# Where the reload of a part's outputs stands among SyncE's transfers, in the expert stage of a convolution, attention and expert-FFN kernel

## The chip, the cores and the metric

The kernel runs on one core of one Trainium2 chip. The core has TensorE (PE: matmuls and weight loads), VectorE (DVE), ScalarE (ACT), GpSimd (POOL) and SyncE (SP), and 16 DMA engines that move data between DRAM and the on-chip memories. SyncE, ScalarE and GpSimd each issue transfers on a queue of their own. The metric is the device time of one execution in microseconds (us), given as the median of several runs.

## The reference

The input x is 32 images of 56 x 56 positions with 128 channels. It goes through a normalisation, a convolution with binarised inputs and weights, windowed attention with 4 heads, and then the part that matters here, an expert layer of 64 experts. Each expert picks the 8 best tokens of each image, pools them, puts the pooled vector through two layers, and adds its output back to the tokens that it picked:

```python
vals, idx = jax.lax.top_k(probs.transpose(0, 2, 1), K)
...
pooled = jnp.einsum('bked,bke->bed', gathered, topv)
...
h = jax.nn.gelu(jnp.einsum('ebd,edh->ebh', h, weight1), approximate=False)
...
out = jnp.einsum('ebh,eho->ebo', h, weight2)
...
weighted = jnp.einsum('beo,bke->bkeo', out, topv).reshape(Bn, K * E, O)
outputs = jnp.zeros((Bn, Sn, O), dtype=x.dtype)
outputs = outputs.at[jnp.arange(Bn)[:, None], flat_idx].add(weighted)
```

A token can be picked by several experts of its image. The result is the attention's output plus these outputs. All of it is float32; the sizes are 8 tokens an expert and image, a hidden width of 512, and 128 channels in and out.

## The kernel before

The first and by far the longest stage is a software pipeline over 112 blocks (16 pairs of images, 7 blocks a pair): convolution, attention, gate logits, and per pair the choice of tokens. It writes the attention's outputs into `out` and, for every chosen token, its row into `grows` and into `share` the weights with which the experts' outputs go into that row (zero for an expert that did not pick it).

The stage that the change touches comes last. The 64 experts are done in `NQ` = 8 parts of 8. For part q these functions are called:

- `load1` (L355) and `load2` (L360) load the two weight matrices of the part's experts, 2048 KB each, into `u1` and `u2` (the profile calls both `u`). Parts 0, 2, 4, 6 and 1, 3, 5, 7 take turns on two sets of buffers, so the weights of part q+2 can only come once part q has read its own.
- `load_rows` (L1053) and `load_shares` (L1057) load `f_rows` and `f_sh`, 1024 KB each: the token rows of the part for all 16 pairs, and their weights. There are four buffers for rows and three for shares.
- `hidden` (L1064) multiplies the pooled vectors with the first weights on TensorE; VectorE copies the result to `hs`.
- `gelus` (L1081) turns `hs` on TensorE (`hT_ps`, L1076) and applies the gelu on ScalarE, 32 instructions a part.
- `outputs` (L1096) multiplies with the second weights; VectorE adds the bias (`os`, L1102), and ScalarE's queue stores the result into `eout` in DRAM (L1104, 128 KB).
- `reload` (L1111) reads `eout` back in two transfers of 64 KB, in the layout that the next step needs: experts on the partitions. The buffer is `eo`, and the profile shows it under the name `logits`, which the same memory had before. Which queue issues the reload is an argument of the function.
- `finals` (L1120) has 16 matrix products of shares and `eo` (32 matmul instructions, `fo`), VectorE adds the token rows to them (L1125), and GpSimd writes the 16 x 128 finished rows to their places in `out` by an indirect transfer for each pair (L1129, 16 a part). The writes of part q+1 to a pair come after those of part q to the same pair, since a token can be in both.

The orders of TensorE, VectorE, ScalarE and SyncE are written out by hand: each of them runs its instructions in the order of the calls, and an instruction that waits holds what is behind it on its engine. In part q TensorE has the turn of `gelus(q)`, then `finals(q - 1)`, then `outputs(q)`, then `hidden(q + 1)`. A reload waits for its store to have landed, and `fo` waits for the reload. The framework adds waits of its own: the transfers of SyncE's and ScalarE's queues take eight semaphores in turn, and each waits until the one before it on its semaphore has landed.

Up to `outputs(0)` nothing differs. Behind it the kernel before has part 0's reload on SyncE's queue and the later ones on ScalarE's, ahead of that part's gelus. Rows and shares are loaded one part ahead, with the first weights of part q+2 ahead of them and the second weights of part q+2 issued behind `outputs(q)`.

Of the kernel before, what the change touches and what calls it, by code (L numbers as in the profile page):

```python
# [30 lines left out]
def kernel(  # L31
# [15 lines left out]
    nc = tc.nc  # L47
# [10 lines left out]
    NQ = 8  # L58
# [308 lines left out]
    def main_loop(fast):  # L367
        with ExitStack() as main:
# [564 lines left out]
            for n in range(-6, N + 1):  # L933
# [34 lines left out]
                if n == N - 4:  # L968
                    parts = [Part(0, early)]
# [79 lines left out]
            def load_rows(q, n0=0, n1=NPAIR):  # L1049

                if n0 == 0:
                    rows[q] = frow.tile([P, NPAIR, P], F32, name="f_rows")
                nc.sync.dma_start(out=rows[q][:, n0:n1], in_=grows[q][:, n0:n1])  # L1053

            def load_shares(q):
                shs[q] = fsh.tile([P, NPAIR, 2, ES], F32, name="f_sh")
                nc.sync.dma_start(out=shs[q], in_=share[q])  # L1057

            def hidden(q):
                part = parts[q]  # L1060
                for g in range(q * GQ, (q + 1) * GQ):
                    hp = eps.tile([P, HF], F32, name="hp")
                    for e in range(EG):
                        nc.tensor.matmul(  # L1064
                            hp[e * B : (e + 1) * B, :], lhsT=pooled[:, g * EG + e, :],
                            rhs=part.u1[:, g * EG + e - q * EP, :], start=True, stop=True,
                        )
                    hs[g] = eh.tile([P, HF], F32, name="hs")
                    nc.vector.tensor_copy(hs[g], hp)

            def gelus(q):
                for g in range(q * GQ, (q + 1) * GQ):
                    hT_ps = eps.tile([P, NHC, P], F32, name="hT_ps")
                    hc = hs[g].rearrange("p (m c) -> p c m", c=NHC)
                    for c in range(NHC):
                        nc.tensor.transpose(hT_ps[:, c, :], hc[:, c, :], ident)  # L1076
                    hT[g] = eh.tile([P, NHC, P], F32, name="hT")
                    for c in range(NHC):
                        for e in range(EG):
                            cols = slice(e * B, (e + 1) * B)  # L1080
                            nc.scalar.activation(  # L1081
                                hT[g][:, c, cols], hT_ps[:, c, cols], AF.Gelu,
                                bias=hbias[:, g * EG + e, c : c + 1],
                            )

            def outputs(q):
                part = parts[q]
                os = eh.tile([P, GQ, P], F32, name="os")
                for g in range(q * GQ, (q + 1) * GQ):

                    op = eps.tile([P, 2, P], F32, name="op")
                    for c in range(NHC):
                        for e in range(0, EG, 2):
                            two = slice(e * B, (e + 2) * B)
                            e0 = g * EG + e - q * EP
                            nc.tensor.matmul(  # L1096
                                op[two], lhsT=hT[g][:, c, two], rhs=part.u2[:, e0 : e0 + 2, c, :],
                                start=(c == 0), stop=(c == NHC - 1),
                            )
                    for e in range(EG):  # L1100
                        one = slice(e * B, (e + 1) * B)
                        nc.vector.tensor_add(os[one, g % GQ], op[one, e % 2, :], obias[one, g])  # L1102
                es = slice(q * EP, (q + 1) * EP)
                nc.scalar.dma_start(  # L1104
                    out=eout[es].rearrange("(g e) b o -> (e b) g o", e=EG), in_=os
                )

            def reload(q, queue):
                es = slice(q * EP, (q + 1) * EP)
                for i in range(2):  # L1110
                    queue.dma_start(  # L1111
                        out=eo[i * E + es.start : i * E + es.stop],
                        in_=eout[es].rearrange("e (i n) o -> i e n o", i=2)[i],
                    )

            def finals(q):
                for a in range(0, NPAIR, FP):
                    fo = eps.tile([P, FP, P], F32, name="fo")
                    for n in range(a, a + FP):
                        nc.tensor.matmul(  # L1120
                            fo[:, n - a, :], lhsT=shs[q][:, n].rearrange("p i s -> p (i s)"),
                            rhs=eo[:, n, :], start=True, stop=True,
                        )
                    row = rows[q][:, a : a + FP]
                    nc.vector.tensor_add(row, fo, row)  # L1125


                for n in range(NPAIR):
                    put = nc.gpsimd.indirect_dma_start(  # L1129
                        out=of, out_offset=bass.IndirectOffsetOnAxis(ap=rowidx[:, n, q : q + 1], axis=0),  # L1130
                        in_=rows[q][:, n, :], in_offset=None,
                    ).ins
                    before = [last[n]] if n in last else []
                    for w in before:
                        tc.add_manual_dep(put, w.name, sync_dep, reason="rows of the same images")
                    tc.declare_no_dep(put, group=puts, keep=before, reason="rows of other images")
                    tc.add_to_no_dep_group(puts, put)
                    last[n] = put
# [30 lines left out]
            load_shares(0)  # L1169
            outputs(0)  # L1170

            hidden(1)
            reload(0, nc.sync)
            load_rows(1)
            load_shares(1)
            parts[2].load2()
            for q in range(1, NQ + 1):
                if q > 1:
                    if q < NQ:
                        hidden(q)  # L1180
                    reload(q - 1, nc.scalar)
                if q + 2 < NQ:
                    parts[q + 2].load1()
                if q + 1 < NQ:
                    load_rows(q + 1)
                    load_shares(q + 1)
                if q < NQ:
                    gelus(q)
                finals(q - 1)
                if q < NQ:  # L1190
                    outputs(q)
                if q + 2 < NQ:
                    parts[q + 2].load2()

    bound_r = nc.values_load(bounded[0:1, 0:1])
    with tc.If(bound_r > 0) as sure:
        main_loop(True)
    with sure.Else():
        main_loop(False)
# [41 lines left out]
```

## Time and profile before

| | us |
|---|---|
| median of 3 runs (2402.36 to 2407.58) | 2405.96 |
| the profiled execution, its own time | 2399.98 |
| its span | 2398.2 |
| TensorE busy in the span | 2164.7 (90%) |
| VectorE busy | 1777.1 (74%) |
| ScalarE busy | 1159.6 (48%) |
| GpSimd busy | 814.3 (34%) |
| first row write of the last stage (L1129) starts | 2198.58 |
| last row write starts | 2390.34 |

The span runs from the first to the last recorded instruction of the profiled execution. Times in the traces are us from its start. The 128 row writes take 0.967 us each of GpSimd's time and follow each other at 1.27 us. Within the stage the DMA queues moved 41.10 MB for SyncE, 8.66 MB for GpSimd and 1.97 MB for ScalarE (2170 to 2400 us).

Four kinds of views are used. A chain of waits follows the work that ended last back in time and gives start, duration, and the engine or transfer that the time went to, with the line. A timeline lists the instructions of one engine or queue (SPq is SyncE's) with start and duration. A wait view gives who waited for whom: total us, times, longest. A window view gives the busy time of each engine in a stretch, then the granted clock of TensorE as a share of full speed, the busy share of the DMA engines and the GB/s that they moved.

### The profile page before, as it was taken

How to read it: one execution, taken by the hardware profiler on the slowest of the kernel's cores; microseconds unless marked ns; L12 is line 12 of the kernel's file. 1: busy time of each engine (PE TensorE's matmuls, PEld its weight loads, DVE VectorE, ACT ScalarE, POOL GpSimd, SP SyncE). 2: the span in 40 equal slices, each digit the busy share in tenths (PEclk: the TensorE clock that was granted, in tenths of full speed). 3: DMA queues.
4: the chain of work that ended last, by engine and by line, in shares of the span. 5: the costliest groups of instructions: out<-in, count | busy, mean ns of one | idle time of the engine just before them, and what ended most of it. 6: DMA issues, size and time to landing. Idle time of an engine off the chain costs nothing.

```text
span 2398.2 us, 82838 instructions
## 1 busy us (share of the span) xinstructions
PE 2164.7 (90%) x35865; PEld 1524.2 (64%) x35865; DVE 1777.1 (74%) x4974; ACT 1159.6 (48%) x1683; POOL 814.3 (34%) x772
## 2 busy tenths in 40 slices
PE   6769999999999999999999999999999999954452
PEld 5656676667676666667676666666666767632332
DVE  7975567788888888888887878787878787775221
ACT  0015555555555556565655565656555555432210
POOL 1012223242424242424242333333333333334556
PEclk9989999999999999999999999999999999977776
DMA  9943464544444445454545363636363535647961
GB/s 367 393 153 84 138 166 101 119 112 107 109 111 105 115 102 118 99 120 97 122 98 122 82 137 80 139 80 139 79 137 81 135 84 127 189 124 259 356 231 58
DMA packets 238300, 334.31 MB, mean 139 GB/s; under 512 B 50598, under 2 KB 175206, under 8 KB 231654
## 3 DMA queue, kind: packets, MB, share of 16 engines
q1 hardware_dynamic: 207878, 254.56, 38.1%
q0 software_dynamic: 27648, 72.38, 13.0%
q8 instruction: 285, 4.67, 0.8%
q10 hardware_dynamic: 2400, 1.97, 0.3%
q14 instruction: 89, 0.73, 0.1%
HBM read 195.14 MB, written 134.74 MB: 138 GB/s over the span
## 4 chain that ended last, share of the span: by engine, by line
PE 77%; ACT 7%; DVE 6%; DMA 5%; issue 3%; POOL 2%; SPq 0%; POOLq 0%; ACTq 0%; DVEq 0%
PE cv L509 8%; PE av L639 8%; PE kT_ps L550 8%; PE pj L673 8%; PE v_ps L566 7%; PE sc L590 6%; PE xT_ps L440 4%; PE lg L701 4%; PE yt L440 4%; ACT bn L488 4%; PE rr L537 4%; PE tt L440 3%; ACT xT L480 3%; DVE st L301 3%; PE sc L579 2%
## 5 line engine op out<-in xcount | busy, mean ns | idle before, releaser
L426 POOL TENSOR_TENSOR ln_rstd<-ln_var,nhalf 128x7 f32<-128x7 f32 x112 | 167.6, 1496 | 924.9 <-DVE ln_var L423 609.4
L480 ACT ACTIVATE xT<-xT_ps,conv_nb 128x896 f32<-128x896 f32 x112 | 112.8, 1007 | 406.4 <-PE xT_ps L440 250.2
L426 POOL TENSOR_TENSOR devs<-ln_var,nhalf 128x7 f32<-128x7 f32 x112 | 165.7, 1479 | 266.4 <-DVE ln_var L423 266.4
L605 ACT ACTIVATE pT<-sc 128x896 f32<-128x896 f32 x224 | 193.2, 915 | 119.9 <-PE sc L590 118.9
L639 PEld LDWEIGHTS av<-vblk,pT 64*64 64x64 f32 x12544 | 195.7, 135 | 86.3 <-ACT pT L605 77.1
L509 PE MATMUL cv<-hbits,wconv 128*128 128x448 f16 x1008 | 233.0, 358 | 11.9 <-DVE s L524 5.6
L566 PEld LDWEIGHTS v_ps<-wqkvT,n1T 128*128 128x128 f32 x1568 | 192.7, 192 | 41.6 <-issue 41.6
L639 PE MATMUL av<-vblk,pT 64*64 64x33 f32 x12544 | 209.7, 221 | 6.2 <-issue 5.2
L679 DVE SCALAR_TENSOR_TENSOR tT<-pj,bproj_c,yT 128x448 f32<-128x448 f32 x224 | 142.7, 678 | 85.0 <-PE pj L673 85.0
L550 PE MATMUL kT_ps<-n1T,wqkvT 128*128 128x448 f32 x448 | 197.6, 563 | 5.5 <-PE aoT_ps L662 1.0
L673 PE MATMUL pj<-aoT,wprojT 64*128 64x448 f32 x896 | 200.2, 566 | 1.1 <-ACT aoT L665 1.1
L522 ACT ACTIVATE s<-cv,conv_mid 128x448 int32<-128x448 f32 x112 | 70.8, 632 | 257.1 <-PE cv L509 257.1
L566 PE MATMUL v_ps<-wqkvT,n1T 128*128 128x128 f32 x1568 | 193.1, 275 | 0.0
L550 PE MATMUL qT_ps<-n1T,wqkvT 128*128 128x448 f32 x448 | 188.1, 542 | 0.1
L692 POOL DMA_DIRECT2D out_dram<-tok x224 | 169.1, 756 | 0.1
L590 PE MATMUL sc<-qT,kT 32*64 32x64 f32 x12544 | 166.9, 233 | 0.0
L433 DVE BATCH_NORM_STATS2 ln_st<-yt 128x6 f32<-128x128 f32 x784 | 164.9, 280 | 2.5 <-PE yt L440 2.5
L590 PEld LDWEIGHTS sc<-qT,kT 32*64 32x64 f32 x12544 | 151.4, 130 | 22.7 <-issue 22.7
L433 DVE BATCH_NORM_STATS2 ln_st<-tok 128x6 f32<-128x128 f32 x784 | 161.8, 278 | 5.0 <-ACT tok L687 4.9
L1129 POOL DMA_INDIRECT out_dram<-f_rows,rowidx x128 | 123.8, 967 | 81.6 <-DVE f_rows L1125 44.7
L488 ACT ACTIVATE bn<-xT_ps,thr_b,thr_a 128x448 f32<-128x448 f32 x224 | 149.3, 720 | 2.6 <-DVE thr_b L330 2.4
L526 DVE SCALAR_TENSOR_TENSOR yT<-s,conv_s,xT 128x448 f32<-128x448 f32 x224 | 143.5, 682 | 4.0
(187 smaller groups left out, 4082.9 us busy)
## 6 DMA issues: line engine op xcount, KB each, us to landing
xb<-in_x_dram SPq DMA_DIRECT2D x16, 3136.0 KB
xb<-in_x_dram SPq DMA_DIRECT2D x224, 224.0 KB
toks<-tok SPq DMA_DIRECT2D x224, 224.0 KB
out_dram<-tok POOLq DMA_DIRECT2D x224, 224.0 KB, 3.5
u<-in_L_ffn_weight_dram SPq DMA_DIRECT2D x16, 2048.0 KB
drow<-devs SPq DMA_DIRECT2D x30, 672.0 KB
share<-zero SPq DMA_DIRECT2D x8, 1024.0 KB
grows<-rows SPq DMA_DIRECT2D x32, 256.0 KB
```

Of the source, the lines that this page charges most:

```text
L426: nc.gpsimd.tensor_tensor(rstd, var, nhalf[:, :n], ALU.pow)
L433: nc.vector.bn_stats(st[:, u, :], src[:, u, :])
L440: nc.tensor.transpose(units(t)[:, u, :], src[:, u, :], ident)
L480: nc.scalar.activation(self.xT.rearrange("c i (p j) -> c i p j", j=NU), units(xT_ps).rearrange("c j (i p) -> c i p j", p=WIN), AF.Identity ...
L488: nc.scalar.activation(bn[:, i].rearrange("c h (g j) -> c h g j", j=NU), units(xT_ps)[:, :, i * WIN : (i + 1) * WIN].rearrange("c j (h g) ...
L509: nc.tensor.matmul(self.cv[:, :BT], lhsT=wconv[:, t, :], rhs=hb[:, r * RB + kh : r * RB + kh + RB, kw : kw + W], start=(t == 0), stop=(t = ...
L550: nc.tensor.matmul(pp[:, a, :BT], lhsT=wqkvT[:, s, :], rhs=flat[:, a * BT : (a + 1) * BT], start=True, stop=True,)
L566: nc.tensor.matmul(units(vp)[:, u, :], lhsT=self.n1T[:, u, :], rhs=wqkvT[:, 2, :], start=True, stop=True,)
L590: nc.tensor.matmul(tiles[h // 2][part, h % 2, u * WIN : (u + 1) * WIN], lhsT=left[hp, u, part], rhs=right[hp, u, part], start=False, stop= ...
L605: nc.scalar.activation(pT, rows2(sc), AF.Exp, scale=HD ** -0.5)
L639: nc.tensor.matmul(av[h % 2 * WIN : (h % 2 + 1) * WIN, i, m * VW : (m + 1) * VW], lhsT=self.pT[h // 2][rows, h % 2, u, :], rhs=self.vb[row ...
L673: nc.tensor.matmul(pj[:, i, :BT], lhsT=wprojT[rows, g, :], rhs=self.aoT[rows, :, g, :], start=(g == 0), stop=(g == 1),)
```

## The change

After the change every reload is issued on SyncE's queue, and each part has one order there: the reload of part q-1, the shares and the rows of part q itself, the second weights of part q+1, the first weights of part q+2. Before, the rows and shares of part q+1 were loaded in part q, on SyncE, without regard to the reload, and the second weights of part q+2 behind `outputs(q)`. The special case for part 1 goes away, and ScalarE's queue keeps only the stores. The amount of data, the number of transfers and all computation stay as they are.

```diff
-            hidden(1)
-            reload(0, nc.sync)
-            load_rows(1)
-            load_shares(1)
-            parts[2].load2()
             for q in range(1, NQ + 1):
-                if q > 1:
-                    if q < NQ:
-                        hidden(q)
-                    reload(q - 1, nc.scalar)
+                if q < NQ:
+                    hidden(q)
+                reload(q - 1, nc.sync)
+                if q < NQ:
+                    load_shares(q)
+                    load_rows(q)
+                if q + 1 < NQ:
+                    parts[q + 1].load2()
                 if q + 2 < NQ:
                     parts[q + 2].load1()
-                if q + 1 < NQ:
-                    load_rows(q + 1)
-                    load_shares(q + 1)
                 if q < NQ:
                     gelus(q)
                 finals(q - 1)
                 if q < NQ:
                     outputs(q)
-                if q + 2 < NQ:
-                    parts[q + 2].load2()
```

## The prediction

> **What bounds the kernel now.** First the shares of the chain of waits over the whole span, and the page's slices of DMA:
>
> ```profile
> PE 77%; ACT 7%; DVE 6%; DMA 5%; issue 3%; POOL 2%; SPq 0%; POOLq 0%; ACTq 0%; DVEq 0%
> DMA  9943464544444445454545363636363535647961
> ```
>
> Up to about 2170 us the chain is TensorE's, and the change touches nothing there. The diff lies in the last 230 us (slices of 60 us each, the last four: 7, 9, 6, 1), where DMA is the busy resource. So I read only the tail. Second, who makes GpSimd wait there, from 2198 us on; its 128 row writes (L1129) are the last work of the kernel:
>
> ```profile
> POOL out_dram L1129 <- DVE f_rows L1125: 44.7, 7, 12.7
> POOL out_dram L1129 <- issue: 32.3, 106, 0.3
> ```
>
> Sixteen writes of a part follow each other at 1.27 us, so a part costs GpSimd 20.33 us. It starts parts 0 to 5 at 2198.58, 2224.31, 2249.90, 2276.62, 2303.65 and 2330.57, and 6 and 7 with no gap. Between parts 0 and 5 it thus waits for 5.57, 5.55, 6.69, 6.97 and 6.90 us (the group's 44.7 less the 12.7 ahead of the first write): 31.7 us is all that can be won while the writes stay as they are. Third, the chain of waits over one such period, which says what it waits for:
>
> ```profile
> 2257.07 9.31 DMA eout<-os
> ...
> 2266.46 0.27 ACTq L1111
> ...
> 2266.77 6.55 DMA logits<-eout
> ...
> 2273.57 5.61 PE fo L1120 x32
> 2279.17 3.65 PE op L1096 x32
> ...
> 2284.07 9.02 DMA eout<-os
> ```
>
> A ring of five links: a part's outputs are stored (eout), reloaded (logits is the old name of the buffer eo), multiplied into rows (fo), and the next part's outputs (op) are only then made. I call R the issue of a reload's first half. On ACT's queue R is 2213.56, 2239.82, 2266.46, 2293.17 and 2320.21: a mean period P of (2320.21 - 2213.56)/4 = 26.66 us, over GpSimd's 20.33. Fourth, why its two transfers are slow. The windows (TensorE, weight load, VectorE, ScalarE, GpSimd busy, then granted clock, DMA share, GB/s):
>
> ```profile
> 2213.00:2240.00 27.00, 12.78 (x88) 9.56 (x88) 6.35 (x14) 5.90 (x32) 16.56 (x18) 0.69 1.03 381
> 2293.00:2320.00 27.00, 12.54 (x88) 9.25 (x88) 6.38 (x14) 5.79 (x32) 15.45 (x16) 0.75 0.85 285
> 2340.00:2357.00 17.00, 10.07 (x67) 8.32 (x65) 5.06 (x12) 5.80 (x32) 13.00 (x14) 0.80 0.22 68
> ```
>
> While 6 MB a part are loaded, DMA is full, and store and reload take 9 and 7 us. In the third row nothing is loaded any more, and the chain there has
>
> ```profile
> 2340.43 3.08 DMA logits<-eout
> ```
>
> Call Y the time from R to the first fo: 7.70, 7.03, 7.11, 7.42 and 7.31 us on ACT's queue under load, 3.64 and 3.99 for the last two, without. Call X the time from the store's issue to R: 7.71, 7.63, 9.39, 9.10 and 9.02 under load, 1.94 and 1.91 without. From the first fo to the next store's issue it is 10.2 to 10.9 us, mean 10.5. P = Y + 10.5 + X. Fifth, the sync queue's own order at the only reload that is on it already:
>
> ```profile
> 2188.37 0.33 SPq L1057 DMA_DIRECT2D f_sh<-share  x1
> 2188.91 0.63 SPq L1111 DMA_DIRECT2D logits<-eout  x2
> 2189.59 0.35 SPq L1053 DMA_DIRECT2D f_rows<-grows  x1
> 2189.99 0.42 SPq L1057 DMA_DIRECT2D f_sh<-share  x1
> 2190.51 0.43 SPq L360 DMA_DIRECT2D u<-in_L_ffn_weight_dram  x1
> 2190.99 6.00 SPq L355 DMA_DIRECT2D u<-in_L_ffn_weight_dram  x1
> ```
>
> This is the pattern that the change gives to every part. The reload stood behind 1.05 MB issued 0.54 us before and ahead of 6.29 MB, and took Y = 2195.51 - 2188.91 = 6.60. 1.05 MB at the 390 GB/s of full windows are 2.7 us; 6.6 - 2.7 = 3.9 is the unloaded 3.8. What is ahead in the queue costs its time; what is behind, nothing that shows.
>
> **The change part by part.** *Reload.* Fourteen issues of about 0.3 us leave ScalarE's queue for SyncE's. ScalarE, which waited some 20 us a part ahead of its gelus (L1081, 5.8 us), runs them earlier. That is worth nothing: they are done before the fo in front of which they stand (2214.52 to 2220.45, fo at 2221.26). On SyncE the reload waits for the store, and everything behind it waits too: shares and rows of part q, second weights of q+1, first weights of q+2, 6.29 MB in four issues (0.35, 0.42, 0.43 and 6.00 us above; SyncE is free again some 8 us after R, long before the next R).
>
> *Are the loads late?* Shares and rows q are needed by fo a period later, second weights by op a period and 13 us later. The tightest are the first weights q+2: needed for L1064 right after the next op, at R + P + 13, or 36 us after R. They land when the batch is through. 2192 to 2276 us moved 361 GB/s, 1.05 MB per 20.33 us (52 GB/s) of it row writes; 6.29 MB at 361 - 52 = 309 GB/s are 20.4 us, at 400 - 52 = 348 (the better windows) 18.1. With some 2.5 us for the reload first, the batch is through at R + 20.6 to R + 22.9. So 13 us of cover remain, and the late issue costs nothing itself. Buffers don't hold either: what the moved loads overwrite was last read a part earlier.
>
> *Reload time Y.* Bounds 3.64 (no load) and 7.70 (as now), nearest row the SyncE one: 3.9 after its backlog is taken off. The batch must be through at the next R for that; I take 3.8.
>
> *Store time X.* The store is issued at R + 3.8 + 10.5 = R + 14.3, into the rest of the batch. Under load it takes 7.6 to 9.4, so the next R is at R + 21.9 to 23.7; when the batch ends first (R + 20.6) and 1.9 us follow, R + 22.5. I take P = 22.5. Bounds: 21.0, for 7.6 MB a part (loads, writes, 0.26 MB of store and reload) at 361 GB/s, and 24.5, for 9.4 + 14.3 and 0.8 us of rest that the reload still finds ahead of it.
>
> *Waits between queues.* The waits of SyncE's queue in the tail have this row:
>
> ```profile
> SPq L1053 <- DMA logits<-eout: 30.6, 3, 13.9
> ```
>
> Rows loads wait for reloads that they share no data with, since the program gives the transfers of both queues eight semaphores in turn and each waits for the eighth before it. After the change a part has seven transfers in one order; the eighth before is a part old and has landed. If a load did wait for its own part's reload, the batch would start 1.3 us later (3.8 for 2.5): P 23.8, within the bounds.
>
> **Sum.** R for part 1 stays at 2213.5 (the same reload ahead of it, the same fo and op, X 7.7 with the batch of 2189 ending by 2212). First write of part 1: 2213.5 + 3.8 + 3.05 (fo to first write, 2273.57 to 2276.62) = 2220.35 against 2224.31. Part 5: 2213.5 + 4 x 22.5 + 6.85 = 2310.35 against 2330.57: 20.2 us earlier. Part 6 loads 4.2 MB, through at R + 14.5, store back by R + 18.3, first write possible 25.2 us after R against 6.85 + 20.33 = 27.2 when GpSimd is free: from part 5 on GpSimd sets the time, as now. Span 2398.2 - 20.2 = 2378.0, that execution 2399.98 - 20.2 = 2379.8. The median of the runs, 2405.96, lies 6.0 above the profiled one: 2385.8, say **2386**. With P 21.0 and 24.5 the gain is 26.2 and 12.2: 2380 to 2394.
>
> **Rivals.**
>
> *GpSimd bound throughout.* If the batch drains before the store is issued, X and Y are both short and P falls under 20.33. Part 5 then starts at 2220.35 + 4 x 20.33 = 2301.7: gain 28.9, **2377**. Against it: 7.6 MB in 20.33 us are 374 GB/s without a pause; only single windows reach that.
>
> *The reload stays slow* (Y 7.3 on either queue): part 1 at 2213.5 + 7.3 + 3.05 = 2223.85, P = 7.3 + 10.5 + 8.5 = 26.3, part 5 at 2329.05, gain 1.5: **2404**. With 1 MB still ahead at each R (Y 6.6) P is 25.6 and the gain 5. For it: six of the eight reloads took over 6.5 us. Against it: the split of the SyncE reload above. The Trainium skill (DMA: Bandwidth & Descriptors, "Issuing engines are not separate DMA queues") speaks for this rival: all issuing engines feed the same 16 DMA engines, and another issuer saves only its issue time. The same page ("Queues, rings and completion order") has each engine take turns between queue rows while one row's ring goes in order; by that the reload loses its turn of its own and must find SyncE's ring empty, which is the condition above, and by it the time is 2386 with an empty ring and 2401 with 1 MB in it. The trace agrees with this second rule where SyncE's reload paid for what was ahead and not for what was behind; no row tells whether ACT's queue alone is what made the others slow.
>
> *Slower: the batch outlasts the store.* DMA now pauses from a batch's end to the next R, and if it moves slowly when batch, writes and store mix, the store, issued into the batch, ends only with it. P is then 2.5 + 6.29 MB / rate + 1.9, over 26.66 once the loads get under 283 GB/s. Windows of 4 us with 251 and 255 GB/s in all lie around the reloads. At 300 in all, 248 for loads: P = 29.8, part 5 at 2339.6, 9.0 late, part 6 one more: **2416**. Against it: 354 to 381 GB/s over whole periods in which DMA was full.
>
> *The change doesn't do what it says*: a shared semaphore holds SyncE as before and the loads run as now. Then nothing moves: 2406.
>
> **How the numbers follow.** Forecast 0.60, GpSimd bound 0.13, slow reload 0.12, outlasting batch 0.11, no effect 0.04. About 0.2% (4.8 us) is what a measurement of this kernel can tell. Faster: 0.60 + 0.13 and a third of the slow reload (its 1 MB form), 0.77; slower 0.11; within 0.12. The range takes the first three cases, 2376 to 2405; the forecast's own is 2380 to 2394.
>
> **What would show it.** Right: reloads on SyncE's queue 3.6 to 4.5 us ahead of fo; R every 21 to 24 us; DMA share near 1 for some 20 us after each R, then a short pause; GpSimd's gaps 1 to 3 us and gone from part 5 on; nothing changed ahead of 2190 us. Wrong: fo 7 us behind R (slow reload), a store of over 12 us (outlasting batch), or TensorE waiting at L1064 or L1096 for weights, which I have priced at nothing.

## The result, and the profile after

| | before | after |
|---|---|---|
| median of the runs, us | 2406.47 (2402.36 to 2407.58) | 2380.15 (2378.07 to 2382.68) |
| the profiled execution, us | 2399.98 | 2378.07 |
| its span, us | 2398.2 | 2376.3 |
| first row write of the last stage (L1129) | 2198.58 | 2199.98 |
| from there to the end of the span | 199.6 | 176.3 |

The kernel is faster: the ratio after to before is 0.9894, 95% interval 0.9877 to 0.9911, or 26 us of 2406 (21 to 30). The stage that the change touches is 23.3 us shorter in the profiled executions; that it began 1.4 us later is not the change's doing, since part 0's reload, ahead of which the programs are the same, was already issued 1.6 us later (2190.48 for 2188.91).

GpSimd's waits in the stage, after (total us, times, longest):

```profile
POOL out_dram L1129 <- issue: 32.9, 108, 0.3
POOL out_dram L1129 <- DVE f_rows L1125: 19.0, 7, 12.5
POOL out_dram L1129 <- DMA out_dram<-f_rows,rowidx: 6.2, 13, 2.6
```

The 44.7 us of before are 19.0, and 12.5 of these are the wait ahead of the very first write; the gap ahead of part 2 stands in the third row, as its longest. The gaps ahead of parts 1 to 5 are 1.90, 2.58, 1.43, 2.05 and 0.42 us, 8.4 in all where there were 31.7. That difference is the 23.3 us. From the first write of part 5 to the end it is 67.6 us in both kernels.

The chain of waits over one period, after, to be set against the one shown of before:

```profile
2236.18 0.30 SPq L1111
...
2236.52 4.83 DMA logits<-eout
...
2241.60 6.43 PE fo L1120 x32
2248.03 3.65 PE op L1096 x32
...
2252.98 6.23 DMA eout<-os
...
2259.26 0.30 SPq L1111
...
2259.61 3.21 DMA logits<-eout
```

The ring is the same, and both of its transfers are shorter: a store of 6.2 us where that chain has 9.0 and 9.3, and reloads of 3.2 and 4.8 us where it has 6.6. SyncE's queue (start, duration, line, transfer):

```profile
2236.18 0.64 SPq L1111 DMA_DIRECT2D logits<-eout  x2
2236.87 0.35 SPq L1057 DMA_DIRECT2D f_sh<-share  x1
2237.26 0.43 SPq L1053 DMA_DIRECT2D f_rows<-grows  x1
2237.79 0.38 SPq L360 DMA_DIRECT2D u<-in_L_ffn_weight_dram  x1
2238.22 5.32 SPq L355 DMA_DIRECT2D u<-in_L_ffn_weight_dram  x1
2259.26 0.64 SPq L1111 DMA_DIRECT2D logits<-eout  x2
```

From 2243.5 to 2259.3 SyncE issues nothing: it stands at the reload and waits until the store has been issued and has landed. DMA has enough to do for most of that time all the same, as the windows over two periods show (columns as before); in windows of 4 us its share dips only just ahead of some reloads, to 0.57 from 2256 to 2260 us.

```profile
2236.00:2259.00 23.00, 13.23 (x88) 10.02 (x88) 6.35 (x14) 5.60 (x33) 15.82 (x17) 0.72 0.97 352
2280.00:2302.00 22.00, 12.15 (x88) 8.85 (x88) 6.35 (x14) 6.34 (x38) 15.46 (x16) 0.81 1.00 363
```

### The profile page after: what moved, and what is told of

Same layout as the page of the kernel before. It is cut to its first block, busy times and chain, and to the rows that moved or that the text cites. A ratio compares the mean times of both kernels' runs of the same rounds, so it can differ in the third digit from the quotient of the medians.

```text
span 2376.3 us, 82834 instructions
## 1 busy us (share of the span) xinstructions
PE 2162.9 (91%) x35865; PEld 1522.2 (64%) x35865; DVE 1778.4 (75%) x4974; ACT 1160.7 (49%) x1683; POOL 814.6 (34%) x772
## 4 chain that ended last, share of the span: by engine, by line
PE 78%; ACT 7%; DVE 6%; DMA 4%; issue 3%; POOL 2%; SPq 0%; POOLq 0%; DVEq 0%
PE cv L509 9%; PE av L639 8%; PE kT_ps L550 8%; PE pj L673 8%; PE v_ps L566 7%; PE sc L590 7%; PE xT_ps L440 4%; PE lg L701 4%; PE yt L440 4%; ACT bn L488 4%; PE rr L537 4%; PE tt L440 3%; ACT xT L480 3%; DVE st L301 3%; PE sc L579 2%
## 5 line engine op out<-in xcount | busy, mean ns | idle before, releaser
L522 ACT ACTIVATE s<-cv,conv_mid 128x448 int32<-128x448 f32 x112 | 70.8, 633 | 257.0 <-PE cv L509 257.0
L1129 POOL DMA_INDIRECT out_dram<-f_rows,rowidx x128 | 123.8, 967 | 58.1 <-issue 32.9
```

## The experiments

Four kernels separate the order of the transfers from the queue and from how far ahead the loads are. Each was run beside the kernel before. Because the stage began between 2197 and 2207 us in different executions, the last column takes the time from the first row write to the end of the profiled span. Y is the time from a reload's issue to fo, X from a store's issue to the next reload, P the period, each for the parts named below; the P of a part runs from its reload to the next part's.

| kernel | ratio to before, 95% interval | stage, us |
|---|---|---|
| before | | 199.6 |
| after | 0.9894 (0.9877 to 0.9911) | 176.3 |
| reloads back on ScalarE's queue | 0.9995 (0.998 to 1.001) | 199.4 |
| before, reloads on SyncE's queue | 0.9962 (0.9947 to 0.9976) | 191.6 |
| after, rows and shares one part ahead | 0.99 (0.9875 to 0.9924) | 179.8 |
| after, loads ahead of the reload | 1.0038 (1.0022 to 1.0053) | 212.6 |

**Reloads back on ScalarE's queue.** The loads keep the order of after among themselves, but no reload in their queue holds them until the store has landed.

```diff
-                reload(q - 1, nc.sync)
+                reload(q - 1, nc.scalar if q > 1 else nc.sync)
```

> The changed kernel, with the reloads of parts 1 to 7 back on ScalarE's queue; SyncE's loads keep their new order but nothing holds them until the store has landed. Order theory (the gain comes from loads that start only behind the reload): the loads start some 8 us ahead of the reload again, Y is back at 7 us, X at 7.5 to 9, P 26, time 2398 to 2407. Rival, later loads (the gain comes from rows and shares being asked for a part later, on whichever queue the reload is): Y 3.8 to 5, P 21.7, time 2378 to 2384.

The ratio is 0.9995: the whole gain is gone. For parts 1 to 5, Y is 7.0 to 7.8 and X 6.6 to 9.2, and P is 24.8 to 27.0 for parts 1 to 4. The chain of waits has, for part 4's reload,

```profile
2294.49 6.54 DMA logits<-eout
```

The rival of later loads falls: the order in which SyncE asks for the loads is that of after, and it brings nothing without the wait in front of them.

**The kernel before, with the reloads on SyncE's queue.** One word.

```diff
-                    reload(q - 1, nc.scalar)
+                    reload(q - 1, nc.sync)
```

> The kernel before with one word changed: the reloads of parts 1 to 7 on SyncE's queue, all loads in the order of before (rows and shares a part ahead, second weights behind the outputs). Order theory: the first weights, rows and shares now stand behind the reload, only the second weights (2.1 MB, 5.4 us at 390 GB/s) come between op and store; they are through before the store has landed, so Y is 3.8 to 4.5, X 7.5 to 9, P 22 to 23.5, time 2381 to 2392. Rival, later loads: rows and shares are a part ahead as before, so P stays 26 and the time 2400 to 2407. Rival, all loads must be behind the reload: half the gain, some 2393.

The gain was 0.4%, some 9 us, where I had expected 14 to 25. Its chain has two reloads of the same size on the same queue:

```profile
2207.21 8.44 DMA eout<-os
...
2216.01 12.18 DMA logits<-eout
...
2238.63 8.42 DMA eout<-os
...
2247.41 3.44 DMA logits<-eout
```

and SyncE's queue ahead of the first of them is

```profile
2190.63 0.35 SPq L1053 DMA_DIRECT2D f_rows<-grows  x1
2191.02 0.43 SPq L1057 DMA_DIRECT2D f_sh<-share  x1
2191.55 0.39 SPq L360 DMA_DIRECT2D u<-in_L_ffn_weight_dram  x1
2191.99 5.80 SPq L355 DMA_DIRECT2D u<-in_L_ffn_weight_dram  x1
2197.83 5.55 SPq L1053 DMA_DIRECT2D f_rows<-grows  x1
2203.43 0.72 SPq L1057 DMA_DIRECT2D f_sh<-share  x1
2205.93 0.38 SPq L360 DMA_DIRECT2D u<-in_L_ffn_weight_dram  x1
2215.67 0.66 SPq L1111 DMA_DIRECT2D logits<-eout  x2
```

Seven loads, 10.5 MB, had been asked for since the reload before, and the rest of them stood ahead: Y = 12.60, and GpSimd's gap ahead of part 1 was 11.63 us, longer than in any part of before. From part 2 on nothing stood ahead, and Y is 3.5 to 3.9. So a place on SyncE's queue is good or bad by what is ahead in it. I had overlooked this first backlog. P is 22.9 to 23.4 between the reloads of parts 2 and 5, above the mean of 21.65 of after, and what is longer is the store: X is 8.1 to 9.6, with 2.1 MB of second weights issued 1.3 us ahead of it.

**Rows and shares one part ahead, behind the reload.**

```diff
-                if q < NQ:
-                    load_shares(q)
-                    load_rows(q)
+                if q == 1:
+                    load_shares(1)
+                    load_rows(1)
                 if q + 1 < NQ:
+                    load_shares(q + 1)
+                    load_rows(q + 1)
                     parts[q + 1].load2()
```

> The changed kernel with rows and shares loaded one part ahead as in the kernel before, everything behind the reload. The first batch is 8.4 MB in place of 6.3. Order theory: the first period is some 4 us longer, the others 21.7, part 5 starts 4 us later than in the changed kernel: 2382 to 2387. Rival, later loads: the gain goes, 2398 to 2407.

As the order theory had it: only the first period changes (Y of part 1 is 8.34, behind the rest of a batch of 8.4 MB in place of 6.3), then Y is 3.8 to 4.6 and X 6.2 to 7.0, and P is 21.0 to 22.0 between the reloads of parts 2 and 5. How far ahead the loads are asked for is not what matters.

**Loads ahead of the reload, all on SyncE's queue.**

```diff
-                reload(q - 1, nc.sync)
+                if q == 1:
+                    reload(q - 1, nc.sync)
                 if q < NQ:
                     load_shares(q)
                     load_rows(q)
...
                     parts[q + 2].load1()
+                if q > 1:
+                    reload(q - 1, nc.sync)
```

> The changed kernel with the four loads of a part ahead of its reload in SyncE's order (parts 1 to 7's reloads), the reload still on SyncE's queue. Order theory: loads start when their buffers are free, some 8 us ahead of the reload; 1.3 to 3.5 MB stand ahead of it in its queue, Y 7 to 13, X 9, P 26 to 32, time 2400 to 2430. Rival, the queue makes the gain (ScalarE need not wait, whatever the order on SyncE): 2378 to 2386.

Slower than before by 0.4%. For parts 1 to 4 Y is 15.6, 7.3, 8.7 and 9.3, X 7.9 to 10.4, P 26.3 to 36.4. The queue, the engine that issues and the loads are those of after, only the order within the queue is not. The chain of waits has, for part 3's reload,

```profile
2288.35 8.20 DMA logits<-eout
```

Together with the run on ScalarE's queue this shows that neither SyncE's queue alone nor the loads' order among themselves brings the gain: the loads have to stand behind the reload. Not tried was a reload on ScalarE's queue with the loads held back until the store has landed, so whether it has to be SyncE's queue that holds them stays open.

**No weight loads.** What is the period of after bound by? Parts 2 to 7 here compute with the weights of parts 0 and 1, so two thirds of a part's loads are left out.

```diff
         def load1(self):
+            if self.q >= 2:
+                return
...
         def load2(self):
+            if self.q >= 2:
+                return
...
-                part = parts[q]
+                part = parts[q % 2]
```

> The kernel without the weight loads of parts 2 to 7 a third time (two thirds of the loads left out), since VectorE stood still on the second chip too. If VectorE does not stand still: DMA theory X 2 to 3, Y 3.8, no gaps on GpSimd ahead of parts 2 to 7, 167 to 169 us from the first row write to the end; chain theory X 6.3, Y 3.8 to 5.4, 175 to 177. If it does: some 213 us as on those two chips.

In this run VectorE did not stand still, unlike in two earlier runs of this kernel, told of below. The ratio is 0.9872 (0.9828 to 0.9915), the stage 169.4 us. The chain (this kernel's lines stand four further down than those of after):

```profile
2242.29 3.43 DMA logits<-eout
...
2245.86 6.35 PE fo L1124 x32
2252.21 3.65 PE op L1100 x32
...
2257.16 2.06 DMA eout<-os
```

Store and reload are at their unloaded lengths, X 1.9 to 2.1 and Y 3.5 to 4.1 from part 1 on; the reloads follow each other every 16.9 to 17.3 us from part 2 on, and GpSimd has no gap over 0.31 us from part 1 on: it alone sets the time. The 6.9 us between 176.3 and 169.4 are thus what the weight loads, 4.2 of a part's 6.3 MB, still cost after the change (by the two ratios, which were measured on different chips and whose intervals overlap, it is 5 us).

**The same kernels on other chips.** On three other chips the kernel before took 2463 to 2468 us. The changed kernel, the kernel without weight loads and two forms meant to be faster still were run there.

> The changed kernel once more, beside the next three on the same chip. All theories: ratio to the kernel before 0.988 to 0.991, part periods 21 to 23 us, GpSimd gaps of 8 us in all.

The ratio was 0.9945 (0.9921 to 0.9968), outside the 0.988 to 0.991 that I had expected, and the stage 213.6 us. In this execution VectorE stood still twice in most parts; its timeline, with the idle time ahead and what ended it in brackets:

```profile
2311.25 1.19 DVE L1102 TENSOR_TENSOR os<-op,drow 32x128 f32<-32x128 f32 x4 [2.21 <-PE op L1096]
2318.39 1.24 DVE L1102 TENSOR_TENSOR os<-op,drow 32x128 f32<-32x128 f32 x4 [5.96 <-remote]
2328.22 1.48 DVE L1069 COPY hs<-hp 128x512 f32<-128x512 f32 x2 [8.59 <-remote]
```

"remote" is a releaser that the trace does not have. The products that the second and third line need had ended on TensorE at 2311.9 and 2313.8 us. The hidden layer's copy at 2328 is then what fo waits for, through the turn by TensorE, and no longer the reload.

> The changed kernel without the weight loads of parts 2 to 7: these parts compute with the weights of parts 0 and 1, so two thirds of the loads are left out. DMA theory (what is left of the ring's period over GpSimd's 20.33 us is the time that 6.3 MB a part take): X 2 to 3, Y 3.8, the ring could run at 17, GpSimd's gaps vanish, 8 us less than the changed kernel: 2369 to 2374. Rival, chain theory (the period of 21.6 is the fixed length of store, reload, fo and op): the gaps stay, 2378 to 2383.

> The kernel without the weight loads of parts 2 to 7 once more (two thirds of the loads left out, parts 2 to 7 compute with the weights of parts 0 and 1); on the chip of the run before, VectorE stood still 6 to 10 us twice a part in every kernel, for a reason that its trace does not name, and that hid the ring. Read from the first row write to the end of the span, which was 199.6 us before the change and 176.3 after it. DMA theory: X 2 to 3, Y 3.8, no gaps on GpSimd, 167 to 169 us. Chain theory: X and Y as after the change, 175 to 177.

Ratios 0.9942 (0.9915 to 0.997) and 0.9914 (0.9882 to 0.9946), stage 215.3 and 216.3 us: with VectorE standing still it made no difference whether two thirds of the loads were there. X was 1.9 to 2.1 and Y 7.7 to 11.3 in parts 1 to 6, Y now with the wait for VectorE in it. These runs say nothing of the ring; the one told of above does.

Two forms take load out of the first three batches: the rows of parts 1 to 3 come early, and in the second form part 0's reload also goes ahead of its shares.

```diff
             pair.put_rows()
+            for q in (1, 2, 3):
+                load_rows(q)
...
-                    load_rows(q)
+                    if q > 3:
+                        load_rows(q)
```

> The changed kernel with the rows of parts 1 to 3 loaded ahead of part 2's first weights, in the stretch from 2172 to 2190 us in which DMA is half idle; batches 1 to 3 are 5.2 MB in place of 6.3. DMA theory: their periods fall from 21.0 to 23.1 to near 20.3, GpSimd's gaps ahead of parts 2 to 4 fall from 6.1 to 1 to 2 us in all: 3 to 5 us less than the changed kernel, ratio to before 0.987 to 0.9885. Rival, chain theory: same as the changed kernel. Other rival: the 3.1 MB hold up the first weights of part 2 and the first reload, and part 0 starts later: slower by 2 to 4.

> The kernel with early rows, and part 0's reload ahead of part 0's shares on SyncE's queue. What is ahead in the queue costs its time: the first reload's Y falls from 6.5 to 3.8, but fo also needs the shares, 1.05 MB and 2.7 us behind it: part 0 starts 0 to 2 us earlier, time 0 to 2 us under the kernel with early rows alone.

> The changed kernel with the rows of parts 1 to 3 loaded ahead of part 2's first weights and part 0's reload ahead of its shares, once more for the same reason. DMA theory: GpSimd's gaps ahead of parts 1 to 4 fall from 8.0 us in all to 2 to 4, from the first row write to the end 171 to 174 us, ratio to before 0.986 to 0.9885. Chain theory: 176, ratio as after the change (0.989).

> Rows of parts 1 to 3 ahead of part 2's first weights and part 0's reload ahead of its shares, a third time. If VectorE does not stand still: DMA theory, GpSimd's gaps ahead of parts 1 to 4 fall from 8.0 us in all to 2 to 4, 171 to 174 us from the first row write to the end (176.3 after the change), ratio to before 0.986 to 0.9885; chain theory 176 and 0.989. If it does: some 212 us and 0.991 to 0.994.

Early rows alone: 0.9961 (0.994 to 0.9982). With the reload first: 0.9942 (0.9915 to 0.9969), 0.9912 (0.9881 to 0.9943) and 0.9932 (0.9906 to 0.9959). In the form with the reload first, the first fo came 6.1 to 6.6 us behind its reload and waited for the shares, which now stand behind it. VectorE stood still in all of them, with gaps of 5 to 8 us on GpSimd ahead of parts 1 to 6, so whether these forms beat the change where it doesn't stand still is open. Where it doesn't, they could win on GpSimd's gaps no more than the 6.9 us that the kernel without weight loads wins.

## Why the prediction was right

2386 us was forecast, a gain of 20, and 2380.15 was measured, a gain of 26.3; in the profiled spans, where the sum was made, it is 21.9, and 23.3 within the stage. The other 4.4 us of the 26.3 are no part of the mechanism: the profiled execution lay 6.5 us under its median before and 2.1 us after. The mechanism was that of the forecast. Two of its terms had errors of opposite sign, and that they partly cancel is luck.

*What bounds it.* The ring through store, reload, fo and op, above GpSimd's 20.33 us: shown. The gaps of GpSimd account for the whole difference, and from part 5 on GpSimd sets the time, as the sum had it (gap 0.42, then 0.30).

*Reload time Y, 3.8.* Measured 3.82, 5.42, 3.80, 4.82 and 3.84 for parts 1 to 5. The two long ones had a rest of the batch ahead: batch 2, from the reload of 2215.17, was still moving at 2237, after the reload of 2236.18 had been issued. The split of before's only SyncE reload into an unloaded time and 2.7 us for the 1 MB ahead fits all of these, and the 12.60 behind a long backlog is the same rule at a larger size. The Trainium skill (DMA: Bandwidth & Descriptors, "Queues, rings and completion order") has each engine consume the descriptors of one row's ring in order. These rows agree with it. That transfers behind a reload cost it nothing also held: three or four loads follow each of the 3.8s.

*Store time X, about 8.2.* This term was mis-sized: 6.28 to 6.73 us was measured. All five loaded stores of before, 7.6 to 9.4, had a second-weights load of 2.1 MB issued 1.2 to 1.3 us ahead of them, because both wait for op; the change moves that load behind the reload. The kernel before with only its reloads moved keeps that load where it was, and it keeps the long store (8.1 to 9.6), while both kernels that issue everything behind the reload have 6.2 to 7.1. I had carried over the store time of a pattern that the change takes apart. That the load ahead of it is the cause is argued, not shown: it was not moved alone, and with the reloads back on ScalarE's queue one store, issued at 2233.95, had that load ahead of it at 2232.67 and took 6.57. A full DMA over the period does not explain the long stores either: the prediction's second window, 2293 to 2320 us, has a share of 0.85, and the store in it took 9.02.

*The period, 22.5.* Measured 21.65 between the reloads of parts 1 and 5: 4.5 for Y, 10.8 from fo to the store and 6.3 for X. The gain on X (1.9) is partly given back by Y (0.7) and by 0.3 us more from fo to the store. The lower bound taken from 7.6 MB at 361 GB/s, 21.0, was the better estimate: the batch of one part fills nearly the whole period.

*Late loads, priced at nothing.* Right: from 2190 us on TensorE's products wait for the reload ahead of fo (61.7 us in 8 waits) and 1.4 us for VectorE ahead of the turns at L1076, and never at L1064 or L1096 for weights. The wait of rows loads for reloads is gone from SyncE's waits, which have 105.3 us in 8 waits at the reload itself.

*ScalarE freed, priced at nothing.* Right, as far as it was tried: ScalarE starts its gelus 4.7 to 5.1 us ahead of the reload now, where it started them some 0.7 to 1 us behind its issue before, and the kernel with the loads ahead of the reload has ScalarE as free and is slower than before.

*The rivals.* The slow reload: the Trainium skill (DMA: Bandwidth & Descriptors, "Issuing engines are not separate DMA queues") speaks of the same 16 engines whoever issues. The runs agree that the issuer by itself decides nothing: on SyncE's queue the ratio is 1.0038 with the loads ahead of the reload, 0.9962 with the loads as before, and 0.9894 with all of them behind it. The change gains because the issuer decides what a transfer stands behind and what its wait holds up. The outlasting batch: the store did not end only with the batch (in the kernel one part ahead it had landed while the next reload still found some 4.5 us of loads), and all transfers together ran at 352 to 363 GB/s. (The 354 to 381 GB/s named against this rival are not all of whole periods: the windows of before with a share of 1.00 to 1.03 have 343 to 381.) GpSimd bound throughout needs the loads to go, which the kernel without weight loads shows.

## What to carry to other kernels

A short transfer that a chain waits for, on a queue full of bulk loads, cost here what was ahead of it in its queue: 3.8 us with nothing there, 6.6 behind 1 MB, 12.6 behind a long backlog. On a queue of its own beside running loads it took 7.0 to 7.8. Letting it hold back the next bulk loads can pay even though their queue then issues nothing, as long as those loads have a period of slack: here SyncE waited 16 us of a period of 23 and nothing came late. Before a transfer time is carried over from a profile, look at what was issued within a microsecond or two ahead of it, and whether the change moves that.

## What the runs showed of the hardware that was not expected

The ratio is 0.9894 where the change was first measured and 0.9945 on another chip, where the kernel before takes 2464 us. The time there is lost ahead of the last stage (first row write at 2226.32 for 2199.98) and in it, where VectorE stands still up to 10 us at a time, in most parts twice, 95 us in all in the changed kernel, with no releaser in the trace. (ScalarE waits in the same way in the first stage, 49.2 us in nine waits at L522.) GpSimd's gaps are then 7 to 8 us in most parts, with or without the weight loads. What holds VectorE there was not found out. The trace does show a coincidence: the copy of the hidden layer starts 1.2 to 2.7 us after the end of the last row write of parts 1 to 5 (2328.22 in the lines above, where part 3's last write ended at 2326.29), so GpSimd's next part, which comes behind that copy, the turn, fo and VectorE's sum, can't follow without a gap. Whether the copy waits for the writes is not shown. A second thing is the store: 128 KB take X = 1.9 us alone, 6.2 to 7.1 beside a running batch, and 7.6 to 10.4, in one case 6.6, when 2 MB are issued 1.2 to 1.3 us ahead of it on another queue.
